# Gating the expert rows where they are made, with the gates carried in the rows of x, and a last stage that adds two gated rows

## The chip, the cores and the metric

One core of a Trainium2 chip. Its engines work side by side, each through its own list of instructions in order: PE (TensorE, matrix products into PSUM), DVE (VectorE), ACT (ScalarE), POOL (GpSimd) and SP, which here only starts transfers. Sixteen DMA engines move data between DRAM and the on-chip memory (SBUF). The time is device microseconds (us) of one execution, and a kernel's time is the median of its runs. Beside the runs there is one profiled execution, which gives the trace.

## The reference

Feature rows x of 6250 nodes (D = 256) go through a graph layer, a mixture of experts, a batch norm and a layer norm:

- x' = gc(x) + x W_res + b: each node sums the scaled rows of its neighbours over 200,000 edges, followed by a product with W_gc.
- Router: logits x' Wg + bg over 64 experts, the two largest, gates g0 and g1 = softmax of the two.
- Expert e on a row: h = gelu(row w1[e] + b1[e]) (512 wide), y = h w2[e] + b2[e] (256 wide).
- core(n) = g0 y0 + g1 y1 for the two experts of node n.
- v = x' + core; mean and variance of v over all nodes, per column; batch norm with gamma and beta.
- Output: layer norm, per row, of x + batchnorm(v).

All values are float32.

## The kernel before, in words

Nodes are numbered in 50 tiles of 125 (`NT`, `TP`). The stages in order:

1. **Graph stage**, to about 950 us: x' is made tile by tile and written to `x_dram` in DRAM; top-2 values and indices are kept in SBUF.
2. **Routing**, to about 1013 us. SP loads all of x' back into `x_all` (L1193, in tens of tiles), DVE makes the gates (L1240, L1241, `gates[:, 2, NT]`), and each token's place in its expert is counted. `table` builds, with one-hot products on PE, for each slot of each expert the token that sits there; `tokens` (L1355 to L1365) turns that into `ids` (the row of x' to fetch) and `dest` (the row of `y_dram` to write: 2 x token + which of its two experts). The gates are multiplied by `valid` (L1374).
3. **Expert stage**, to about 1475 us. 64 experts in turns, each with 80 to 416 slots, in blocks of 128 slots; 124 blocks in all. For a block POOL gathers rows of x' (`rows_in`, indirect DMA, four experts ahead), PE transposes them (`turned_in`), DVE adds a bias on the way out of PSUM (`xgT`), PE makes the first layer in four pieces (`ph`, 4 matmuls each), ACT applies Gelu (`hT`), PE makes the second layer (`py`, 8 matmuls for a block), DVE adds b2 (`ys`, L1462), and POOL scatters the rows to `y_dram` (L1463). SP loads the weights two to three experts ahead. PE, ACT, DVE and SP keep the order in which `slotted` writes the work down: per turn two pieces of the next expert's first layer, the transposes of the one after it, then blocks of the second layer and the remaining pieces in alternation. In each fourth turn DVE subtracts a column mean `c0` from four tiles of `x_all` (L1506), 13 times in all; this centres the batch norm's sums. POOL adds beta to rows of x meanwhile (L1513).
4. **Last stage.** `joined` loads, for two tiles at a time, the two expert rows of each token (`yr`, 2 KB a token, 8 buffers), ACT multiplies one by its gate (L1590), DVE multiplies the other and adds it to x (L1592), then adds the first (L1594). `summed` squares the result on ACT (L1599), and PE sums over the nodes with a matrix of ones: the values into `pm` (L1601), the squares into `pv` (L1603), two accumulations over all 50 tiles. Then come mean, variance and `scale` (L1613 to L1623), and the norm of the rows, group by group, with the stores of the output.

DRAM stores of 125 rows are cut in 112 and 13 rows by `node_dma`. All of the last stage stands in written order.

Of the kernel before, what the change touches and what calls it, by code (L numbers as in the profile page):

```python
# [25 lines left out]
N = 6250  # L26
# [37 lines left out]
OPENING = 40  # L64
SIZES_OUT = [1, 2, 3] + [6] * 6 + [4, 3, 1]
# [85 lines left out]
def gnn_moe_kernel(ctx, tc, x_in, x_cols, src, dst, bases, nexts, firsts, parts, lasts, W_gc, b_gc, W_res, b_res, Wg, bg, w1, b1, w2, b2,  # L151
# [53 lines left out]
    x_dram = dram.tile([N, D], F32, name="x_dram")  # L205
# [35 lines left out]
    with tc.tile_pool(name="edges", bufs=1) as ep, ExitStack() as later:  # L241
# [352 lines left out]
        with tc.tile_pool(name="xs", bufs=1) as xs, tc.tile_pool(name="hotg", bufs=2) as hg, \  # L594
# [246 lines left out]
            def x_step(c, t):  # L841
# [6 lines left out]
                if u == 0 and "x" in live:  # L848
                    t0, z, xr = live["x"]
                    live["steps"] = x_make(z, xr, 2, node_rows(x_dram, t0, 2))  # L850
# [172 lines left out]
            with tc.For_i(0, NT, 1) as ti:  # L1023
# [4 lines left out]
                for run in x_make(z, xr, 1, rows_at(x_dram)):  # L1028
                    run()
# [20 lines left out]
    gates = rpool.tile([TP, 2, NT], F32, name="gates")  # L1050
# [54 lines left out]
    with tc.tile_pool(name="xw", bufs=1) as xw, tc.tile_pool(name="xl", bufs=3) as xl, \  # L1105
# [42 lines left out]
        with tc.manual_schedule():  # L1148
# [38 lines left out]
            node_dma(nc.sync, False, x[:, ta:tb, :], node_rows(x_dram, ta, tb - ta))  # L1187
            for a, b in ((0, ta), (tb, NT)):
                for t0 in range(a, b, 10):
                    n = min(10, b - t0)  # L1190
                    node_in(x_all[:, t0:t0 + n, :], x_dram[:, :], t0, n, ta)
# [48 lines left out]
    V.tensor_mul(gates[:, 1, :], g2, g1)  # L1240
    V.tensor_copy(gates[:, 0, :], g1)  # L1241
# [113 lines left out]
    def tokens(pool, id_t, id_p, dump, n, ids, dest):  # L1355
# [7 lines left out]
        V.tensor_copy(ids, idp)  # L1363
        V.scalar_tensor_tensor(idp, idf, 0.0, dump, op0=ALU.is_equal, op1=ALU.mult)
        V.scalar_tensor_tensor(dest, idf, -1.0, idp, op0=ALU.add, op1=ALU.add)  # L1365

    with tc.tile_pool(name="rt2", bufs=2) as rt2, \
# [5 lines left out]
        for a, b, o in spans:  # L1373
            V.tensor_mul(gates[:, :, a:b], gates[:, :, a:b], valid[:, :, o:o + b - a])  # L1374
        tokens(rt, id_t, id_p, dump, COLS, ids, dest)
# [18 lines left out]
    with tc.tile_pool(name="ex", bufs=2) as xp, \  # L1394
# [33 lines left out]
        def turned_in(xgs, m):  # L1428
# [24 lines left out]
        def second_layer(w2s, b2s, hT, to, m, static):  # L1453

            def block(k):
                n = min(128, m - k * 128)
                py = ps_y.tile([128, D], F32, name="py")
                for c in range(4):
                    T.matmul(py[:n], hT[:, c, k * 128:k * 128 + n], w2s[:, c, :], start=(c == 0),  # L1459
                             stop=(c == 3))  # L1460
                ys = xp.tile([128, D], F32, name="ys", bufs=6)
                V.tensor_add(ys[:n], py[:n], b2s[:n])  # L1462
# [8 lines left out]
        def expert(at, idc, to, m):  # L1471
            w1s, b1_e = first_weights(at)
            w2s, b2s = second_weights(at)
            hT, pieces = first_layer(w1s, b1_e, turned_in(rows_in(idc, m, False), m), m)
            for run in pieces + second_layer(w2s, b2s, hT, to, m, False):
# [5 lines left out]

# [261 lines left out]
```

## Time and profile before

| | us |
|---|---|
| median of 3 runs | 1600.42 (1599.77 to 1601.79) |
| the profiled execution | 1588.94 |
| its span, first to last instruction | 1587.2 |
| PE busy | 1405.6 (89%) |
| DVE busy | 1039.2 (65%) |
| ACT busy | 734.7 (46%) |
| POOL busy | 784.7 (49%) |

The span is what the trace shows; the execution's own time is 1.7 us longer. A busy PE is one with a matmul under way, and matmuls overlap. In rows of the stretches each engine has its busy time and, in brackets, its number of instructions; PEclk is the granted share of TensorE's clock, the DMA share is that of the 16 DMA engines, and the last figure is GB/s. In rows of groups stand line, engine, operation, output and inputs, shape and count, then busy time and the mean of one in ns, and behind the second bar the idle time ahead of them with who ended it. In rows of the timeline: start, duration, engine, line, and in brackets the idle time before. PEld is PE's loading of weights, SPq an instruction of SP's list.

### The profile page before, as it was taken

To read this page: it belongs to the slowest core of one execution; us is meant where nothing else is said; L and a number is where in the kernel's file an instruction comes from. 1 tells how busy PE (TensorE), PEld (TensorE's weight loads), DVE (VectorE), ACT (ScalarE), POOL (GpSimd) and SP (SyncE) were. 2 spreads that over 40 slices of the span, in tenths; PEclk is the share of its full clock that TensorE was granted. 3 is DMA by queue.
4 is the path that set the end of the run, shared out by engine and by line. 5 is a ranking of instruction groups with operands and counts; after the bars stand their busy time and mean duration, and the time that the engine had idled before them with its cause. 6 is when DMAs were issued, how large, how long until landed. Compare 5 with 4: busy or idle time off the path is not lost. (4 is left out here: it accounts for less than half of the span.)

```text
span 1587.2 us, 33048 instructions
## 1 busy us (share of the span) xinstructions
PE 1405.6 (89%) x9969; PEld 1156.2 (73%) x9969; DVE 1039.2 (65%) x2926; ACT 734.7 (46%) x1884; POOL 784.7 (49%) x883
## 2 busy tenths in 40 slices
PE   5999478888899999999999976689999999999893
PEld 2555367777778888999999975678788877777661
DVE  8999988788788887887777738522222233222687
ACT  3676543355555556565555533322222222222667
POOL 5000226766666666666667621255556666554000
PEclk8999699999999999999999996799999999999987
DMA  6899655767677777787777738176678787686725
GB/s 185 263 283 328 238 180 165 198 185 202 186 200 213 214 196 220 200 217 201 219 207 208 215 108 283 55 239 214 224 230 265 255 263 255 202 247 212 265 86 152
DMA packets 209124, 336.40 MB, mean 212 GB/s; under 512 B 22259, under 2 KB 140693, under 8 KB 208937
## 3 DMA queue, kind: packets, MB, share of 16 engines
q1 hardware_dynamic: 154084, 180.30, 36.1%
q0 software_dynamic: 47952, 146.83, 32.6%
q10 hardware_dynamic: 6900, 7.07, 1.6%
q8 instruction: 81, 1.33, 0.4%
q14 instruction: 107, 0.87, 0.2%
HBM read 254.55 MB, written 73.10 MB: 206 GB/s over the span
## 5 line engine op out<-in xcount | busy, mean ns | idle before, releaser
L614 POOL DMA_INDIRECT r<-h_dram,srcg x445 | 474.1, 1065 | 277.9 <-PE pc L700 99.0
L746 PE MATMUL sm<-hrow,counts 128*128 128x258 f32 x1470 | 489.9, 347 | 10.4 <-DVE counts L737 10.2
L720 ACT CAST counts<-pc 128x196 f32 (+7 forms) x879 | 356.6, 406 | 255.3 <-PE pc L700 134.4
L747 PE MATMUL sm<-hrow,counts 128*128 128x256 f32 x1470 | 396.8, 283 | 0.0
L700 PE MATMUL pc<-hotk,lo 128*128 128x245 bf16 (+7 forms) x1118 | 305.3, 304 | 55.6 <-DVE counts L737 17.7
L746 PEld LDWEIGHTS sm<-hrow,counts 128*128 128x128 f32 x1470 | 288.5, 196 | 37.4 <-issue 19.9
L687 DVE TENSOR_TENSOR hotk<-key,iota_h 128x784 bf16<-128x784 f16 (+4 forms) x488 | 247.5, 507 | 87.4 <-PE pc L700 50.8
L747 PEld LDWEIGHTS sm<-hrow,counts 128*128 128x128 f32 x1470 | 281.9, 192 | 1.3
L1449 ACT ACTIVATE hT<-ph,b1c 128x112 f32<-128x112 f32 (+16 forms) x256 | 106.8, 428 | 348.7 <-PE ph L1447 236.2
L737 DVE TENSOR_TENSOR counts<-pc,counts 128x49 f32 x908 | 217.9, 240 | 52.9 <-issue 10.2
L1459 PE MATMUL py<-w2s,hT 128*128 128x256 f32 (+7 forms) x992 | 241.2, 386 | 0.1
L1447 PE MATMUL ph<-xgT,w1s 128*128 128x112 f32 (+17 forms) x1024 | 207.3, 346 | 11.9 <-issue 9.4
L1447 PEld LDWEIGHTS ph<-xgT,w1s 128*128 128x128 f32 x1024 | 169.8, 194 | 44.4 <-issue 22.7
L1459 PEld LDWEIGHTS py<-w2s,hT 128*128 128x128 f32 (+7 forms) x992 | 162.7, 172 | 43.7 <-issue 3.6
L1412 POOL DMA_INDIRECT y_dram<-ys,dest x124 | 119.2, 961 | 138.9 <-DVE ys L1462 77.2
L1462 DVE TENSOR_TENSOR ys<-py,b2s 128x256 f32<-128x256 f32 (+7 forms) x124 | 51.8, 421 | 165.3 <-PE py L1459 112.6
L700 PEld LDWEIGHTS <-lo 128*128 128x128 bf16 x1118 | 100.8, 101 | 80.9 <-issue 22.4
L1437 DVE TENSOR_SCALAR xgT<-pte,bsum 128x112 f32<-128x112 f32 (+14 forms) x128 | 48.9, 424 | 167.4 <-PE pte L1434 74.2
L619 PE MATMUL pg<-r,hot 128*128 128x258 f32 x445 | 145.7, 328 | 12.4 <-issue 9.2
L1412 POOL DMA_INDIRECT xg<-x_dram,ids x124 | 119.3, 962 | 41.4 <-issue 26.7
L620 PE MATMUL pg<-r,hot 128*128 128x256 f32 x445 | 125.9, 283 | 0.0
L619 PEld LDWEIGHTS pg<-r,hot 128*128 128x128 f32 x445 | 86.0, 193 | 22.2 <-issue 17.3
(332 smaller groups left out, 1728.7 us busy)
## 6 DMA issues: line engine op xcount, KB each, us to landing
w1s<-in_L_gnn_w_dram SPq DMA_DIRECT2D x64, 512.0 KB
w2s<-in_L_gnn_w_dram SPq DMA_DIRECT2D x64, 512.0 KB
y_dram<-zeros SPq DMA_DIRECT2D x48, 256.0 KB
yr<-y_dram SPq DMA_DIRECT2D x22, 512.0 KB
b2s<-in_L_gnn_b_dram SPq DMA_DIRECT2D x64, 128.0 KB
h_dram<-hrow SPq DMA_DIRECT2D x5, 1536.0 KB
r<-h_dram,srcg POOLq DMA_INDIRECT x445
f<-in_x_cols_dram SPq DMA_DIRECT2D x25, 256.0 KB
```

What stands on the lines that cost most here:

```text
L614: G.indirect_dma_start(out=f32(r[:, :2 * D]), out_offset=None, in_=h_dram[:, :], in_offset=bass.IndirectOffsetOnAxis(ap=idx, axis=0))
L619: T.matmul(pg, hot, r[:, D:], start=first, stop=False)
L620: T.matmul(pg[:, :D], hot, r[:, :D], start=False, stop=last)
L687: V.tensor_tensor(hot, pairs(key, e, n, m), iota_h[:, None, :m, :].to_broadcast([128, n // 2, m, 2]), ALU.is_equal)
L700: T.matmul(pc, los[g // PAIRS][:, r // 2, :, r % 2], hots.pop(g), start=(i == 0), stop=(i == k - 1))
L720: put = S.copy(counts[c % 2][:, :, 1:][:, :, ds(at, w - 1)], pc[:, :, 1:])
L737: add = V.tensor_tensor(to, more, f32(had), ALU.add).ins
L746: T.matmul(sm, by, hrow[:, t, D:], start=(t == 0), stop=False)
L747: T.matmul(sm[:, :D], by, hrow[:, t, :D], start=False, stop=(t == NS - 1))
L1412: w = G.indirect_dma_start(**kw)
L1447: T.matmul(ph[:, :m], w1s[:, kk, c * 128:(c + 1) * 128], xgT[:, kk, :m], start=(kk == 0), stop=(kk == 1))
L1459: T.matmul(py[:n], hT[:, c, k * 128:k * 128 + n], w2s[:, c, :], start=(c == 0), stop=(c == 3))
```

## The change

- `x_dram` gets two columns more: a row is 258 floats. Once the gates are made (now `[125, NT, 2]`), SP stores them from SBUF into these columns, one DMA of 125 x 50 pieces of 8 bytes. Reads and writes of x' use the first 256 columns. The gather of a block brings 258 floats.
- `tokens` also makes `mine_of`: for each slot two 0/1 numbers that say whether it is the token's first or second choice (one product and two comparisons on DVE). The multiplication of the gates by `valid` goes.
- `turned_in` makes, per block, the slot's gate as the sum of the two carried gates times those two numbers (one small DVE instruction with an accumulator).
- `second_layer`: DVE adds b2 (into `yb`), ACT multiplies by the slot's gate into `ys`, which is scattered, and DVE adds the gated rows to `y_sum` (one tile of 128 x 256 for all blocks).
- In each fourth turn DVE also adds the centred tiles of x into `x_sum` (4 tiles wide); at turn 52 `x_sum` is folded into `y_sum`. POOL zeroes both beforehand.
- Last stage: `pm` is one matmul over `y_sum`, and `mean` and `msq` are made ahead of the loop. `joined` takes groups of 1, 1, 2, eleven times 4, and 2 tiles (4 buffers of 4 tiles), with one DMA for each (the last group has its last tile apart), and only adds the two rows to x, on DVE. `summed` squares a group on ACT and sums the squares on PE, in the same turn as its group.

```diff
+SIZES_IN = [1, 1, 2] + [4] * 11 + [2]
-    x_dram = dram.tile([N, D], F32, name="x_dram")
+    x_dram = dram.tile([N, D + 2], F32, name="x_dram")
+    x_rows = x_dram[:, :D]
...
-    V.tensor_mul(gates[:, 1, :], g2, g1)
-    V.tensor_copy(gates[:, 0, :], g1)
+    V.tensor_mul(gates[:, :, 1], g2, g1)
+    V.tensor_copy(gates[:, :, 0], g1)
+    w = nc.sync.dma_start(out=node_rows(x_dram[:, D:], 0, NT), in_=gates)
+    for u in loads:
+        tc.declare_no_dep(w.ins, u.ins, reason="other columns of x_dram")
+    G.memset(y_sum, 0.0)
+    G.memset(x_sum, 0.0)
...
         V.tensor_copy(ids, idp)
+        odd = pool.tile([128, n], F32, name="odd")
+        V.scalar_tensor_tensor(odd, idp, -2.0, idf, op0=ALU.mult, op1=ALU.add)
         V.scalar_tensor_tensor(idp, idf, 0.0, dump, op0=ALU.is_equal, op1=ALU.mult)
         V.scalar_tensor_tensor(dest, idf, -1.0, idp, op0=ALU.add, op1=ALU.add)
+        for j in range(2):
+            V.tensor_scalar(mine[:, :, j], odd, float(j + 1), None, op0=ALU.is_equal)
...
-        for a, b, o in spans:
-            V.tensor_mul(gates[:, :, a:b], gates[:, :, a:b], valid[:, :, o:o + b - a])
...
-                xg = gx.tile([128, D], F32, name="xg")
+                xg = gx.tile([128, D + 2], F32, name="xg")
...
+            for k, xg in enumerate(xgs):
+                n = min(128, m - k * 128)
+                two = gx.tile([128, 2], F32, name="two")
+                V.scalar_tensor_tensor(two[:n], xg[:n, D:], 1.0, mine[k][:n], op0=ALU.mult, op1=ALU.mult,
+                                       accum_out=gate[k][:n])
             return xgT
...
+                yb = xp.tile([128, D], F32, name="yb", bufs=3)
+                V.tensor_add(yb[:n], py[:n], b2s[:n])
                 ys = xp.tile([128, D], F32, name="ys", bufs=6)
-                V.tensor_add(ys[:n], py[:n], b2s[:n])
+                S.activation(ys[:n], yb[:n], AF.Copy, scale=gate[k][:n])
+                V.scalar_tensor_tensor(y_sum[:n], yb[:n], gate[k][:n], y_sum[:n], op0=ALU.mult, op1=ALU.add)
...
                     V.tensor_tensor(xs, xs, c0[:, None, :].to_broadcast([TP, min(4, NT - e), D]), ALU.subtract)
+                    V.tensor_tensor(x_sum[:, :min(4, NT - e)], x_sum[:, :min(4, NT - e)], xs, ALU.add)
+                if e == NT + 2:
+                    V.tensor_tensor(x_sum[:, :2], x_sum[:, :2], x_sum[:, 2:], ALU.add)
+                    for j in range(2):
+                        V.tensor_tensor(y_sum[:TP], y_sum[:TP], x_sum[:, j], ALU.add)
...
-    with tc.tile_pool(name="fin", bufs=1) as fp, tc.tile_pool(name="gat", bufs=8) as gp, \
+    with tc.tile_pool(name="fin", bufs=1) as fp, tc.tile_pool(name="gat", bufs=4) as gp, \
...
+        T.matmul(pm, ones[:, :TP], y_sum, start=True, stop=True)
         mean = fp.tile([TP, D], F32, name="mean")
         V.tensor_scalar(mean, pm, 1.0 / N, None, op0=ALU.mult)
         msq = fp.tile([TP, D], F32, name="msq")
         V.tensor_mul(msq, mean, mean)
+
+        def joined(t0, n):
+
+            yr = gp.tile([128, 4, 2, D], F32, name="yr")
+            loads.clear()
+            node_in(yr[:, :n].rearrange("p t j d -> p t (j d)"), y_rows, t0, n)
+            for u in written[-AHEAD:-1] if t0 == 0 else ():
+                tc.add_manual_dep(loads[0].ins, u.name, SYNCED, reason="the last writes")
+            for j in range(2):
+                V.tensor_tensor(x[:, t0:t0 + n, :], x[:, t0:t0 + n, :], yr[:TP, :n, j, :], ALU.add)
+
+        def summed(t0, n):
+
+            sq = fl.tile([TP, 6, D], F32, name="o")
+            S.activation(sq[:, :n], x[:, t0:t0 + n, :], AF.Square)
+            for t in range(t0, t0 + n):
+                T.matmul(pv, ones[:TP, :TP], sq[:, t - t0, :], start=(t == 0), stop=(t == NT - 1))
+
+        t0 = 0
+        for n in SIZES_IN:
+            joined(t0, n)
+            summed(t0, n)
+            t0 += n
```

The old `joined` and `summed`, with the gate multiplications and the 50 matmuls into `pm`, go.

More of the change, by code (lines that the diff above doesn't have):

```diff
@@ L1027, in gnn_moe_kernel @@
                 z, xr = x_load(rows_at(z_dram), rows_at(r_dram), 1)
-                for run in x_make(z, xr, 1, rows_at(x_dram)):
+                for run in x_make(z, xr, 1, rows_at(x_rows)):
                     run()
@@ L1049, in gnn_moe_kernel @@
     dest = rpool.tile([128, COLS], I32, name="dest")
-    gates = rpool.tile([TP, 2, NT], F32, name="gates")
+    gates = rpool.tile([TP, NT, 2], F32, name="gates")
+    mine_of = rpool.tile([128, COLS, 2], F32, name="mine_of")
+    gate_of = rpool.tile([128, COLS], F32, name="gate_of")
+    y_sum = rpool.tile([128, D], F32, name="y_sum")
+    x_sum = rpool.tile([TP, 4, D], F32, name="x_sum")
     c0 = rpool.tile([TP, D], F32, name="c0")
@@ L1353, in table, with tokens @@
                     T.matmul(id_p, q_p[:, i // 2, :, i % 2], cols[:, i // 2, :, i % 2], **edge)
-    def tokens(pool, id_t, id_p, dump, n, ids, dest):
+    def tokens(pool, id_t, id_p, dump, n, ids, dest, mine):
         idp = pool.tile([128, n], F32, name="idp")
@@ L1372, in gnn_moe_kernel @@
         table(rt2, id_t, id_p, blk_b, COLS)
-        for a, b, o in spans:
-            V.tensor_mul(gates[:, :, a:b], gates[:, :, a:b], valid[:, :, o:o + b - a])
-        tokens(rt, id_t, id_p, dump, COLS, ids, dest)
+        tokens(rt, id_t, id_p, dump, COLS, ids, dest, mine_of)
         pn = ps_l.tile([128, 1], F32, name="pn")
@@ L1451, in first_layer, with second_layer @@
             return hT, [lambda c=c: piece(c) for c in range(4)]
-        def second_layer(w2s, b2s, hT, to, m, static):
+        def second_layer(w2s, b2s, hT, to, gate, m, static):
             def block(k):
@@ L1469, in second_layer, with expert @@
             return [lambda k=k: block(k) for k in range(len(to))]
-        def expert(at, idc, to, m):
+        def expert(at, idc, to, mine, m):
+            gate = [xp.tile([128, 1], F32, name="gate_e")]
             w1s, b1_e = first_weights(at)
             w2s, b2s = second_weights(at)
-            hT, pieces = first_layer(w1s, b1_e, turned_in(rows_in(idc, m, False), m), m)
-            for run in pieces + second_layer(w2s, b2s, hT, to, m, False):
+            hT, pieces = first_layer(w1s, b1_e, turned_in(rows_in(idc, m, False), m, mine, gate), m)
+            for run in pieces + second_layer(w2s, b2s, hT, to, gate, m, False):
                 run()
@@ L1480, in columns, with turned @@
             return [tab[:, c + k:c + k + 1] for k in range(n)]
+        def turned(e, xgs):
+            c, n, m = _place(turns[e])
+            return turned_in(xgs, slots_of_turn[e], [mine_of[:, c + k, :] for k in range(n)], columns(gate_of, e))
         slots_of_turn = [_place(r)[2] for r in turns]
```

56 lines of the change are left out of this document (18 added, 38 removed).

## The prediction

> **What bounds the kernel now.** I read the page first (which engine is full), then the busy time by stretches (which engine is full where), the chain that ended last (what sets the end of the last stage), the groups of that stage, and the timeline around the two seams. The change touches three places: the routing that ends near 1015 us, the expert stage up to 1475 us, and the first part of the last stage.
>
> ```profile
> span 1587.2 us, 33048 instructions
> ...
> core 0: us, PE busy (x) PEld busy (x) DVE busy (x) ACT busy (x) POOL busy (x), PEclk, DMA share, GB/s
> 1000.00:1005.00 5.00, 3.14 (x41) 2.87 (x40) 5.00 (x8) 3.35 (x3) 0.00 (x0) 0.85 0.00 0
> 1100.00:1470.00 370.00, 364.41 (x1892) 292.83 (x1891) 100.43 (x270) 86.94 (x212) 217.26 (x213) 0.99 0.75 237
> 1478.00:1488.00 10.00, 7.96 (x18) 4.18 (x18) 4.08 (x9) 4.94 (x10) 0.00 (x0) 0.66 0.78 245
> 1488.00:1498.00 10.00, 9.41 (x44) 8.22 (x45) 9.28 (x19) 9.54 (x22) 0.00 (x0) 1.00 1.05 392
> 1498.00:1508.00 10.00, 10.00 (x48) 8.72 (x47) 9.37 (x20) 8.93 (x20) 0.00 (x0) 1.00 1.05 387
> 1508.00:1518.00 10.00, 10.00 (x48) 8.72 (x47) 9.37 (x20) 9.04 (x20) 0.00 (x0) 1.00 0.86 290
> 1518.00:1528.60 10.60, 10.60 (x50) 9.20 (x50) 5.30 (x11) 5.00 (x11) 0.00 (x0) 1.00 0.01 2
> ```
>
> Routing (1000 to 1005) is full on DVE, the expert stage (1100 to 1470) on PE with DVE 27% and ACT 23% busy, and the joining of the two expert rows of each token (1488 to 1528.6) is full on PE from 1498 on. There, though, nothing is far behind: DVE and ACT are 90% busy and the DMA engines saturated at 390 GB/s until the reads run out. The chain confirms that PE ends it:
>
> ```profile
> 1475.05 2.69 DMA y_dram<-ys,dest
> ...
> 1481.24 5.84 DMA yr<-y_dram
> ...
> 1490.58 0.86 PE pv L1603 x4
> ...
> 1527.70 0.88 PE pm L1601 x4
> 1528.60 0.43 DVE mean L1613
> 1529.06 0.43 DVE msq L1615
> 1529.60 0.44 DVE scale L1617
> ```
>
> Two tiles cost 0.86 us in `pm` and 0.86 in `pv`, taking turns to the end. The 50 tiles are 25 such pairs: 25 x 1.72 = 43 us of PE.
>
> **The join, part by part.** The rows that carry the terms:
>
> ```profile
> L1592 DVE SCALAR_TENSOR_TENSOR x_all<-yr,gates,x_all 125x256 f32<-125x256 f32 x50 | 21.9, 479 | 4.7 <-DMA yr<-y_dram 4.7
> L1594 DVE TENSOR_TENSOR x_all<-x_all,yr 125x512 f32<-125x512 f32 x25 | 17.3, 692 | 2.6
> L1590 ACT ACTIVATE yr<-yr,gates 125x256 f32<-125x256 f32 x50 | 22.6, 496 | 4.5 <-DMA yr<-y_dram 4.3
> L1599 ACT ACTIVATE sq<-x_all 125x512 f32<-125x512 f32 x25 | 15.7, 627 | 4.3 <-DVE x_all L1594 2.1 <-PE pv L1603 1.8 <-DVE x_all L1592 0.3
> L1639 DVE TENSOR_TENSOR x_all<-x_all,scale 125x1024 f32<-125x1024 f32 x1 | 1.2, 1216 | 0.0
> ```
>
> PE loses `pm` for all tiles but one matmul on `y_sum`, and keeps 25 x 0.86 = 21.5 us. ACT loses the 50 gate multiplications (22.6) and keeps the squares (15.7, less in larger pieces). DVE trades 21.9 + 17.3 = 39.2 us for two additions a group: 2 x 1.216 = 2.43 for each of the 11 groups of four, 2 x 0.69 for each of the two groups of two, 2 x 0.43 (the chain's 256-wide rows) for each of the two single tiles, 31.2 in all. So PE goes from 43 to 21.5, ACT from 38 to 16, DVE from 39 to 31. What is late next is the DMA. By the stretches it moved 2.45 + 3.92 + 3.87 + 2.90 = 13.1 MB from 1478 on; at 390 GB/s the 2.90 MB behind 1508 take 7.4 us, so the last row landed near 1515.4. A group of four is 128 x 4 x 2 KB = 1.05 MB, 2.69 us at that rate, against DVE's 2.43, so DVE keeps up. Four buffers of four tiles hold what eight of two held. A buffer comes free 2.5 us after its group has landed, while three groups (8 us) are still queued, so the reads don't starve.
>
> The end then follows from the last landing. The expert stage ends 0.5 us later (below), which puts it at 1515.9; larger first loads may win up to 1 us of the slow start (245 GB/s in 1478 to 1488), which I keep for the range. The last group (two tiles, 0.51 MB) lands 1.3 us behind its predecessor, so that one landed at 1514.6. DVE adds it until 1517.0 and the last until 1518.4. The square of four (about 0.9 to 1.05, estimated from L1599's 0.627 for half as much) is done by 1518.0, its four matmuls at 1.72 by 1519.8, the last square by 1519.1, the last two matmuls by 1520.7. `mean` and `msq` have been made long before, from `y_sum`, so `scale` starts at 1520.8 instead of 1529.60: 8.8 us sooner.
>
> That takes PE at full clock. PE would be busy 1.72 of each 2.69 us, 64%. The nearest row is 1000 to 1005, where PE is busy 3.14 of 5.00 us (63%) and the granted clock is 0.85, not 1.00. At 0.85 the last six tiles take 3.0 instead of 2.6 us; at half clock 5.2. I take 0.85, the row with the same load: 8.3 us sooner, with 6.2 as the bad end. The Trainium skill (TensorE: Matmul & The Clock Gate, Part 1: The HAM clock gate) says that the clock is halved only behind an idle window of about 3.4 us; PE would idle about 1 us at a time here, so by that rule it stays full and the gain is 8.8. The row of 1000 to 1005 speaks against it, and I go by the row.
>
> Everything behind `scale` stays as it is: the same chain, 58 us to the end.
>
> **The expert stage.** Each of the 124 blocks gets a second DVE pass over 256 (summed gated rows), a small DVE product with its accumulator, and an ACT multiplication between DVE and the scatter; 13 times DVE adds four tiles of x into `x_sum` behind the subtraction that is there already.
>
> ```profile
> L1462 DVE TENSOR_TENSOR ys<-py,b2s 128x256 f32<-128x256 f32 x69 | 29.2, 423 | 83.3 <-PE py L1459 62.1 <-PE ph L1447 13.4 <-issue 4.6
> L1506 DVE TENSOR_TENSOR x_all<-x_all,c 125x1024 f32<-125x1024 f32 x12 | 14.6, 1215 | 0.0
> L1217 DVE COPY b1c<-b1T 128x4 f32 x60 | 11.1, 184 | 4.9 <-issue 1.2 <-ACT hT L1449 0.5
> ...
> L1459 PE MATMUL py<-w2s,hT 128*128 128x256 f32 x528 | 129.9, 390 | 0.0
> ...
> L1447 PE MATMUL ph<-xgT,w1s 128*128 128x160 f32 x80 | 13.2, 303 | 0.0
> ...
> PEld py L1459 <- DVE ys L1462: 1.2, 5, 0.4
> ...
> PE ph L1447 <- ACT hT L1449: 1.8, 3, 0.8
> ```
>
> On DVE: 124 x (0.48 by L1592 + 0.25, estimated from the 0.18 of L1217 and an accumulator read) + 13 x 1.2 = 106 us; on ACT 124 x 0.50 by L1590 = 62 us. Spread over 450 us this takes DVE from 27 to about 50% and ACT from 23 to 37%: there is room, and PE's waits for both were 3 us in the whole stage. What counts is order. DVE and ACT work in order, so a scaled row that waits for DVE holds the next Gelu behind it on ACT, and PE waits for that Gelu one turn later. A block of `py` is 8 matmuls, 129.9 / 528 x 8 = 2.0 us; a piece of `ph` is 4, 13.2 / 80 x 4 = 0.7 us at 160 rows. In an ordinary turn DVE has two `xgT` (about 0.9 us, estimated as two passes like L1462's) and 2 x 0.25 us to do behind the transposes, and is ready before the first `py` ends: no loss. In each fourth turn it also has 1.2 + 1.2 us; the row of the first `py` is then made at about 4.2 to 4.6 us from the transposes, scaled at 5.1, and the two Gelus queued behind it are done at 5.9. PE asks for them behind its `py`, `ph` pieces (two of this turn, two of the next) and transposes: with two blocks 2 x 2.0 + 4 x 0.7 + about 0.4 = 7.2 us, with one block 5.2, and then it loses up to 0.7 to 1.2 us (the pieces of a small expert are shorter). 18 of 64 turns have one block, so about 4 of the 13 heavy turns: at most 4.8, and I take 1.5 us. The bounds are nothing (all hidden) and 13 x 1.2 = 15.6 (each addition shows in full); I stay near the low end because PE's waits for DVE were 1.2 us although the subtraction of the same length stood in that place. POOL's scatters start about 0.6 us later each, its gathers are four turns ahead, so nobody waits for that but the end: the last scatter has ACT's 0.50 in its path, the 0.5 us of above.
>
> **Routing and the gate store.**
>
> ```profile
> 977.12 0.35 SPq L189 DMA_DIRECT2D x_all<-x_dram  x1
> ...
> 978.20 0.41 SPq L1215 DMA_DIRECT2D w1s<-in_L_gnn_w_dram  x1
> ...
> 1012.29 0.23 DVE L159 TENSOR_SCALAR idp<-idp 128x124 f32<-128x124 f32 x1
> ...
> 1012.81 0.29 DVE L1364 SCALAR_TENSOR_TENSOR idp<-idf,dump 128x124 f32<-128x124 f32 x1
> ...
> 1013.57 0.24 POOL L1389 TENSOR_SCALAR below<-pidx 128x1 f32<-128x1 f32 x1 [53.87 <-DVE dest L1365]
> ...
> 1014.85 1.06 POOL L1412 DMA_INDIRECT xg<-x_dram,ids  x1 [0.17 <-issue]
> ...
> L1374 DVE TENSOR_TENSOR gates<-gates,valid x3: 161/197/203, 985.7 to 993.0; 125x48 f32<-125x48 f32 x1, 125x44 f32<-125x44 f32 x1, 125x8 f32<-125x8 f32 x1
> ...
> q1 hardware_dynamic: 430, 0.08, 20.3%
> ...
> q10 hardware_dynamic: 260, 0.26, 15.2%
> ```
>
> POOL starts the gathers behind DVE's last step of `tokens`; that gets `odd` (0.29) and two comparisons (0.23 each), 0.75 us, and DVE, which is full here, loses the three products of L1374, 0.56 us: +0.2. The two memsets on POOL lie in its 53.87 us of idleness.
>
> The gates go to DRAM as 6250 pieces of 8 bytes, on SP's queue between the last load of x (977.12) and the first weights (978.20), and every gather now waits until they have landed. The trace has no such store. The row of 430 packets (the 2 us from 24 us on, nearly all under 512 bytes, reads) gives 20.3% of 32 engine-us = 6.5, 15 ns a packet. The row of 260 (the 5 us from 1013, two loads of 125 rows of 1 KB with ten packets more, which I read as five engines reporting for each load) gives 15.2% of 80 = 12.2, 47 ns a packet. On five engines the store has 1250 packets each: 19 us by the first row, 59 by the second; on 16 it would be 6. I take 19, the row of like size. With 4 to 5 us of loads ahead of it, it ends near 1001, 13 us before the first gather asks; the first three experts' weights behind it (3.4 MB, about 9 us) land by 1010 and are wanted from 1020 on. Cost 0 then, and 24 us if a piece costs 47 ns (end at 1039).
>
> **Sum.** -8.3 (join, with the late last scatter in it) + 1.5 (expert stage) + 0.2 (routing) = -6.6 us. The profiled execution took 1588.94 us (span 1587.2 and 1.7 around it), so 1582.3 in its terms; the median of the runs was 1600.42, 11.5 above that one execution, and I carry the difference over: 1593.8.
>
> **Rivals.** (1) PE's clock: PE runs the join at half clock for most of it. Two tiles then take 1.72 us in `pv` alone, 43 us as before, and only the halves at full clock gain. For: 0.66 in 1478 to 1488, 0.85 at 63% load. Against: a PE that falls behind is busy without pause, and at 100% the rows show 1.00. With half the stretch slow, the join gains 4: about 1598. (2) The gate store is late. The Trainium skill (DMA: Bandwidth & Descriptors, Specifications) says that under 512 bytes the DMA engine reads, modifies and writes; nothing shown here has such a store. The place is the first gather at 1014.85, and the point from which it decides is 26 ns a piece ((1014.85 - 982) / 1250); from 31 ns on the kernel is slower. At 47 ns it costs 24 us: 1618. For: both bounds lie around that point. Against: the 4- to 256-byte packets of the trace cost 15. (3) DVE and ACT show in the expert stage: every heavy turn loses 1.2 us, 15.6 us instead of 1.5: 1608. For: PE is 98% busy, so each wait counts. Against: the two waits above, and DVE half idle.
>
> **Chances.** Forecast 0.65, rival 1 0.12, rival 2 0.13, rival 3 0.10. The forecast's own range is 1590 (start-up gained, expert stage free, full clock) to 1597.5. The whole range, 1588.5 to 1602.5, takes in rival 1 and leaves out most of rivals 2 and 3. 0.2% (3.2 us) is about what a measurement of this kernel can tell from no change. Faster by more: 0.60 of the forecast, 0.06 of rival 1, a little of rival 3's mild end; slower: most of rivals 2 and 3.
>
> **What would show it.** Right: no `pm` of 50 tiles, reads near 390 GB/s from start to end of the join, `scale` some 8 us sooner after the last scatter than 1529.60 - 1475.05 = 54.6 us, PE idle between groups. Gathers that start within 1 us of 1014.85 clear the store; PE's waits for DVE and ACT in the expert stage under 5 us clear that. Wrong: a pause on POOL before the first gather, `pv` at 0.8 us a tile, or the stage from the first gather to the last scatter longer than 460 us by more than 5.

## The result and the profile after

The changed kernel takes 1618.56 us (1613.30 to 1622.69, 5 runs) against 1600.42 (1599.74 to 1605.62, 5 runs): 1.0104 times the time before, with a 95% interval of 1.0084 to 1.0123. It is 18 us slower where 6.6 us of gain were forecast. Its profiled execution took 1618.23 us. The profiled execution of before (1588.94) lay 11.5 us under its own median, so the stages below are also held against a second profile of the kernel before, of 1600.75 us, from the experiments (`same_before`). (Of the executions in the experiments one, of `spread_3`, took 2260.56 us at a granted clock of 0.555, and its ratio leaves it out.) The three marks of `same_before`, from the timeline (first gather, last scatter, `scale`):

```profile
1027.19 1.06 POOL L1412 DMA_INDIRECT xg<-x_dram,ids  x1 [0.16 <-issue]
...
1485.83 0.86 POOL L1412 DMA_INDIRECT y_dram<-ys,dest  x1 [0.85 <-DVEq L1534]
...
1541.37 0.42 DVE L1617 SCALAR_TENSOR_TENSOR scale<-pv,msq 125x256 f32<-125x256 f32 x1
```

The seams of the changed kernel, in the same view: the gate store, the first weight load behind it, and the end of the routing.

```profile
992.42 0.29 SPq L1249 DMA_DIRECT2D x_dram<-gates  x1
993.49 16.21 SPq L1222 DMA_DIRECT2D w1s<-in_L_gnn_w_dram  x1
...
1028.82 0.25 POOL L1403 TENSOR_SCALAR below<-pidx 128x1 f32<-128x1 f32 x1 [53.01 <-DVE mine_of L1381]
...
1030.10 1.06 POOL L1426 DMA_INDIRECT xg<-x_dram,ids  x1 [0.17 <-issue]
```

SP stands for 16 us in the issue behind the store, whose 6250 packets run from 995.9 to 1011.0 us, 19 us ahead of the first gather. POOL waits for DVE's last step (`mine_of`), not for a transfer: the store holds nothing up here. Then the busy time by stretches, the expert stage first and then the join:

```profile
span 1616.6 us, 33281 instructions
...
1030.10:1509.30 479.20, 449.23 (x2264) 357.64 (x2264) 217.54 (x714) 155.90 (x381) 270.55 (x260) 0.97 0.71 221
1512.00:1522.00 10.00, 6.04 (x9) 2.60 (x10) 2.41 (x8) 1.90 (x3) 0.00 (x0) 0.66 0.61 212
1522.00:1532.00 10.00, 8.84 (x20) 5.68 (x20) 8.98 (x10) 3.68 (x5) 0.00 (x0) 0.51 1.01 358
1532.00:1542.00 10.00, 8.36 (x36) 6.30 (x35) 9.18 (x8) 3.71 (x4) 0.00 (x0) 0.98 1.05 386
1542.00:1552.00 10.00, 6.56 (x28) 4.54 (x26) 7.56 (x7) 3.42 (x4) 0.00 (x0) 1.00 1.00 356
```

The expert stage in `same_before`, in the same view:

```profile
1027.00:1486.00 459.00, 441.13 (x2264) 355.30 (x2264) 122.03 (x326) 107.13 (x257) 266.09 (x262) 0.98 0.73 230
```

From first gather to last scatter the expert stage takes 479.2 us, where before took 460.2 and, in `same_before`, 458.6: 20 us are lost here, with DVE only 45% busy. Some 8 of them are longer busy time of PE, 12 are idle time (30.0 instead of 17.5 us). The join is no longer full on PE, and its transfers run at 356 to 386 GB/s, except in the first ten microseconds (212). The chain shows what holds them up:

```profile
1509.34 2.93 DMA y_dram<-ys,dest
1512.27 1.47 issue
1513.74 5.34 PE pf L1610 x6
1519.08 0.45 PE pm L1616 x2
...
1519.55 0.44 DVE mean L1618
...
1520.01 0.42 DVE msq L1620
1520.43 0.35 DVE x_all L1630
...
1521.26 4.92 DMA yr<-y_dram
...
1558.91 0.44 DVE scale L1648
```

DVE, in order, makes `mean` and `msq` ahead of the first addition, and they wait for `pm` behind six `pf` matmuls. So the first addition comes 11.0 us behind the last scatter, and no buffer is free before it. In `same_before` it came 6.3 us behind the last scatter:

```profile
1492.17 0.48 DVE L1592 SCALAR_TENSOR_TENSOR x_all<-yr,gates,x_all 125x256 f32<-125x256 f32 x1 [2.47 <-DMA yr<-y_dram]
```

`scale` starts 49.6 us behind the last scatter instead of 55.5: 6.0 us of gain (5.0 against the first profile of before, with 54.6). From there to the end nothing changed (57.6 and 57.7 us). The groups, with the sizes of the new instructions:

```profile
L1483 ACT ACTIVATE ys<-yb,gate_of 128x256 f32<-128x256 f32 x69 | 35.1, 508 | 140.6 <-DVE yb L1481 109.6 <-issue 28.4 <-DVE two L1455 1.6
L1484 DVE SCALAR_TENSOR_TENSOR y_sum<-yb,gate_of,y_sum 128x256 f32<-128x256 f32 x69 | 33.5, 486 | 2.4
...
L1630 DVE TENSOR_TENSOR x_all<-x_all,yr 125x1024 f32<-125x1024 f32 x22 | 26.9, 1225 | 4.6 <-DMA yr<-y_dram 4.2
...
L1535 DVE TENSOR_TENSOR x_sum<-x_sum,x_all 125x1024 f32<-125x1024 f32 x12 | 14.7, 1225 | 0.5
```

Each is as long as it was costed (0.50, 0.48, 1.22). And the waits of PE (total in us, times, longest):

```profile
PEld py L1478 <- ACT hT L1468: 12.7, 11, 5.1
...
PE py L1478 <- ACT hT L1468: 8.3, 5, 4.7
...
PEld py L1478 <- DVE yb L1481: 3.2, 7, 1.0
```

PE now waits for Gelu's result in front of `py`. The first two rows in `same_before`:

```profile
PEld py L1459 <- ACT hT L1449: 3.8, 3, 2.6
...
PE py L1459 <- ACT hT L1449: 2.6, 3, 2.2
```

Behind such waits its clock is halved for a while (28 us of the stage instead of 15, which makes 0.97 instead of 0.98 in the mean), so that its busy time grows too, from 441.1 in `same_before` to 449.2 us.

### The profile page after: what moved, and what is told of

Same layout as the page of the kernel before. It is cut to its first block, busy times and chain, and to the rows that moved or that the text cites. A ratio compares the mean times of both kernels' runs of the same rounds, so it can differ in the third digit from the quotient of the medians.

```text
span 1616.6 us, 33281 instructions
## 1 busy us (share of the span) xinstructions
PE 1398.0 (86%) x9871; PEld 1137.2 (70%) x9871; DVE 1126.6 (70%) x3269; ACT 760.5 (47%) x1948; POOL 791.4 (49%) x885
## 5 line engine op out<-in xcount | busy, mean ns | idle before, releaser
L748 PE MATMUL sm<-hrow,counts 128*128 128x258 f32 x1470 | 489.8, 347 | 15.6 <-DVE counts L739 12.5
L1478 PE MATMUL py<-w2s,hT 128*128 128x256 f32 (+7 forms) x992 | 246.8, 391 | 18.3 <-ACT hT L1468 8.3
L1483 ACT ACTIVATE ys<-yb,gate_of 128x256 f32<-128x256 f32 (+7 forms) x124 | 63.0, 508 | 236.8 <-DVE yb L1481 177.8
L1481 DVE TENSOR_TENSOR yb<-py,b2s 128x256 f32<-128x256 f32 (+7 forms) x124 | 52.1, 420 | 128.5 <-PE py L1478 77.7
L1468 ACT ACTIVATE hT<-ph,b1c 128x112 f32<-128x112 f32 (+16 forms) x256 | 100.9, 420 | 86.2 <-PE ph L1466 41.1
L1451 DVE TENSOR_SCALAR xgT<-pte,bsum 128x112 f32<-128x112 f32 (+14 forms) x128 | 48.8, 423 | 128.7 <-PE pte L1448 47.5
```

Of the source, the lines that this page charges most:

```text
L748: T.matmul(sm, by, hrow[:, t, D:], start=(t == 0), stop=False)
```

## The experiments

Two kinds of chips turned up, and the numbers can't be read without that: on some (that of the result above and two others) the kernel before takes 1600 to 1603 us, on another 1531 to 1532. Each ratio is to the kernel before on the same chip. The table has the time of each run, its ratio with interval, and from its profile (whose own time stands first) the stages: start of the first gather, from there to the last scatter, from there to `scale`.

| kernel | time | ratio (95%) | profile | gather at | expert | to scale |
|---|---|---|---|---|---|---|
| *before at 1600 to 1603* | | | | | | |
| before | 1600.42 | | 1588.94 | 1014.85 | 460.2 | 54.6 |
| same_before | 1600.86 | 1.0000 (0.9982-1.0017) | 1600.75 | 1027.19 | 458.6 | 55.5 |
| after | 1618.56 | 1.0104 (1.0084-1.0123) | 1618.23 | 1030.10 | 479.2 | 49.6 |
| no_x_sum | 1610.27 | 1.0041 (1.0022-1.0060) | 1610.73 | 1029.80 | 471.4 | 49.2 |
| late_scale | 1605.48 | 1.0018 (0.9996-1.0039) | 1606.68 | 1030.73 | 467.1 | 49.4 |
| late_mean | 1618.77 | 1.0102 (1.0073-1.0131) | 1620.37 | 1030.13 | 483.2 | 47.5 |
| early_gate_3 | 1607.68 | 1.0030 (1.0010-1.0049) | 1604.53 | 1031.11 | 465.2 | 48.8 |
| spread_3 | 1611.60 | 1.0054 (1.0035-1.0073) | 1610.72 | 1030.72 | 471.9 | 49.2 |
| all_three_2 | 1597.58 | 0.9970 (0.9951-0.9989) | 1601.44 | 1027.38 | 467.6 | 47.3 |
| *before at 1531 to 1532* | | | | | | |
| same_before_2 | 1532.21 | 1.0002 (0.9989-1.0015) | 1532.03 | 978.20 | 440.7 | 54.0 |
| wide_rows | 1531.46 | 1.0001 (0.9991-1.0011) | 1533.51 | 979.03 | 440.8 | 54.2 |
| wide_rows_2 | 1532.04 | 1.0000 (0.9986-1.0014) | 1531.22 | 977.42 | 440.4 | 54.0 |
| same_after | 1527.59 | 0.9973 (0.9962-0.9984) | 1531.48 | 978.75 | 444.6 | 48.9 |
| early_gate | 1527.52 | 0.9978 (0.9966-0.9990) | 1529.22 | 979.25 | 440.9 | 49.8 |
| early_gate_2 | 1527.38 | 0.9968 (0.9953-0.9984) | 1530.21 | 980.74 | 441.1 | 49.3 |
| spread | 1529.05 | 0.9987 (0.9976-0.9997) | 1530.28 | 980.04 | 441.6 | 49.6 |
| spread_2 | 1528.25 | 0.9973 (0.9961-0.9985) | 1531.79 | 982.32 | 440.8 | 49.2 |
| late_scale_no_x_sum | 1527.77 | 0.9976 (0.9963-0.9989) | 1528.68 | 979.35 | 441.2 | 48.8 |
| no_y_sum | 1529.80 | 0.9981 (0.9970-0.9993) | 1527.70 | 977.11 | 440.5 | 49.3 |
| all_three | 1525.09 | 0.9950 (0.9932-0.9968) | 1525.09 | 977.11 | 440.0 | 48.0 |

**The kernel before, again (`same_before`).** No edit.

> The kernel before, unchanged, for a second profile. The profiles shown so far put its first gather at 1014.85 us, and that of the changed kernel at 1030.10, though the graph stage is hardly touched. Theory 1 (the one profiled execution of before was a quick one; it lay 11.5 us under its own median): the first gather now comes at 1022 to 1028, the stage from first gather to last scatter again takes 458 to 463 us, and 112 us follow. Theory 2 (the wider rows of x cost the graph stage 15 us): the first gather stays within 3 us of 1015.

The first gather came at 1027.19: the quick profile of before had its 12 us in the graph stage, and the change's 15 us of delay there were mostly that. Theory 1 holds. What is left is 2.9 us, of which the routing (from the last copy of the gates to the first gather) has 42.1 - 41.3 = 0.8; the other 2.1 lie ahead of it and were not explained. With 20.6 more in the expert stage and 6.0 less behind it, the 2.9 make up the 17.5 us between the two profiled executions.

**Without the additions into x_sum (`no_x_sum`).**

```diff
-                    V.tensor_tensor(x_sum[:, :min(4, NT - e)], x_sum[:, :min(4, NT - e)], xs, ALU.add)
```

> The changed kernel without the 13 additions of centred tiles into x_sum, so the mean lacks x (that part of the computation is left out). Theory A (the third rival of the prediction: DVE's second long instruction in each fourth turn delays the rows, ACT and then PE): the stage from first gather to last scatter falls from 479 to 464 to 467 us, and the time by 12 to 15, to about 1605. Theory B (what costs is the gate multiplication that stands ahead of a Gelu on ACT in every block): at most 3 us go, 1615 to 1619. Theory C (DVE's and ACT's added instructions cost little, and the difference is the spread of the graph stage): no change.

Theory A asked for 12 to 15 us off the stage and got 8; the time is 1.0041 of before instead of 1.0104. The long stretch on DVE is a cause, and not the only one.

**The gate multiplication behind the next Gelu (`late_scale`).** A block is cut in two, and its second half (ACT's multiplication, DVE's sum, the scatter) is written behind the next piece.

```diff
+                return lambda: gated(k, n, yb, ys)
+
+            def gated(k, n, yb, ys):
                 S.activation(ys[:n], yb[:n], AF.Copy, scale=gate[k][:n])
...
-                    for run in second[k:k + 1] + first[2 + k:3 + k]:
+                    late = [run() for run in second[k:k + 1]]
+                    for run in first[2 + k:3 + k]:
+                        run()
+                    for run in late:
                         run()
```

> The changed kernel with ACT's gate multiplication of a block, DVE's sum and the scatter written behind the next piece's Gelu instead of ahead of it; nothing is left out. Theory B (a Gelu waits on ACT behind a scaled row, which waits for DVE): PE's waits of 20 us for hT in the expert stage fall to about 5, the stage from 479 to about 465 us, the time to 1603 to 1607. Theory A (DVE's long instructions): the row is late all the same, and the Gelu gets ahead of it only in the heavy turns; a gain of 3 to 8 us, since in those turns too the Gelu no longer waits. Theory C: no change.

The stage fell to 467.1 and the time to 1605.48, as theory B had it, though every instruction is still there. In the waits of this kernel PE's for Gelu went from 12.7 and 8.3 us to:

```profile
PEld py L1478 <- ACT hT L1468: 5.2, 5, 1.6
...
PE py L1478 <- ACT hT L1468: 3.1, 4, 1.2
```

So the larger cause is ACT's order: the Gelu that PE needs stood behind a row that DVE had not yet made.

**`mean` and `msq` behind the first four tiles (`late_mean`).**

```diff
-        T.matmul(pm, ones[:, :TP], y_sum, start=True, stop=True)
-        mean = fp.tile([TP, D], F32, name="mean")
-        V.tensor_scalar(mean, pm, 1.0 / N, None, op0=ALU.mult)
-        msq = fp.tile([TP, D], F32, name="msq")
-        V.tensor_mul(msq, mean, mean)
...
             summed(t0, n)
             t0 += n
+            if t0 == 4:
+                T.matmul(pm, ones[:, :TP], y_sum, start=True, stop=True)
+                mean = fp.tile([TP, D], F32, name="mean")
+                V.tensor_scalar(mean, pm, 1.0 / N, None, op0=ALU.mult)
+                msq = fp.tile([TP, D], F32, name="msq")
+                V.tensor_mul(msq, mean, mean)
```

> The changed kernel with the matmul into pm, mean and msq moved behind the first four tiles of the join; nothing is left out. Theory D (DVE, in order, waits for pm, which stands behind six pf matmuls at half clock, before its first addition, and the four buffers then hold up the reads): the first addition comes at about 6.5 us from the last scatter's start instead of 11.1, and the last scatter to scale takes 46 to 47 us instead of 49.6; time 3 to 4 us less, about 1615. Rival: the first reads or the rate of 390 GB/s set the end, and nothing is gained.

The timeline of this kernel (last scatter, first addition, `scale`), and the first ten microseconds of its reads:

```profile
1513.37 0.86 POOL L1426 DMA_INDIRECT y_dram<-ys,dest  x1 [0.93 <-DVEq L1567]
...
1520.12 0.88 DVE L1625 TENSOR_TENSOR x_all<-x_all,yr 125x256 f32<-125x256 f32 x2 [1.99 <-DMA yr<-y_dram]
...
1560.90 0.42 DVE L1649 SCALAR_TENSOR_TENSOR scale<-pv,msq 125x256 f32<-125x256 f32 x1 [2.79 <-PE pv L1632]
```

```profile
1516.00:1526.00 10.00, 6.57 (x12) 2.92 (x12) 3.14 (x7) 2.95 (x5) 0.00 (x0) 0.66 0.75 260
```

The first addition now waits for its transfer (6.75 us behind the scatter), the reads run at 260 instead of 212 GB/s, and `scale` comes at 47.5 instead of 49.6. Theory D holds in its place with 2.0 us, short of its price (46 to 47). The time doesn't show it: the interval of four runs (1.0073 to 1.0131) is too wide for 2 us, and the expert stage of this profile was 4 us longer, which nothing in the edit explains.

**Both edits of the expert stage (`late_scale_no_x_sum`), and the rows and the store alone (`wide_rows`, `wide_rows_2`).** The latter is the kernel before with the wide rows and the store alone; `pair` is a copy of the gates made for the store:

```diff
-    x_dram = dram.tile([N, D], F32, name="x_dram")
+    x_dram = dram.tile([N, D + 2], F32, name="x_dram")
...
+    V.tensor_mul(pair[:, :, 1], g2, g1)
+    V.tensor_copy(pair[:, :, 0], g1)
+    w = nc.sync.dma_start(out=node_rows(x_dram[:, D:], 0, NT), in_=pair)
...
-                xg = gx.tile([128, D], F32, name="xg")
+                xg = gx.tile([128, D + 2], F32, name="xg")
```

> Both edits at once: the gate multiplication behind the next Gelu, and no additions into x_sum (the mean lacks x: that part is left out). Alone they took the expert stage from 479 to 467 and to 471 us. If the two are separate costs (12 and 8 us), the stage comes back to 459 to 460, that of before, and the time to about 1597. If they are one cost that shows twice (a late row of a heavy turn holding up a Gelu), the stage stays at 465 to 467 and the time at 1603 to 1605.

> The kernel before with only the 1032-byte rows of x_dram, the gathers of 258 floats and the store of the gates in 6250 pieces; the carried gates are read by nobody, and all else is as before. Theory W (wider rows cost: writes of x in the graph stage, unaligned reads in the expert stage): the first gather some 2 to 3 us later than 1027.2, the expert stage up to 4 us longer than 458.6, time 1604 to 1608. Rival (rows and store are free, as the prediction had it): within 1.5 us of the kernel before.

> The kernel before with the rows of 1032 bytes and the store of the gates alone, for a run beside a kernel before of about 1600 us. The changed kernels reached the last step of the gates at 985.8 to 989.7 us there, the kernel before at 973.0 and 985.9. Theory W (wider rows cost where the pauses are): gates at 988 to 990, 1.0015 to 1.003 of the kernel before. Rival (rows and store are free, as beside 1531): 0.999 to 1.001.

All three fell on the quicker chip. There rows and store are free (1.0001 and 1.0000), as forecast; beside 1600 they were not measured. With both edits the expert stage took as long there as that of the kernel with wide rows (441.2 and 440.8). That doesn't tell two separate costs from one that shows twice, for perhaps nothing is lost there even without the edits. The next run asks that.

**The changed kernel again (`same_after`).** No edit.

> The changed kernel, unchanged. In the first profiles SP's plain register instructions (0.01 to 0.05 us as a rule) took over 0.3 us in 32 to 47 of 365 cases of the expert stage, with all engines late around them; in the profiles of wide_rows, early_gate and spread, where the kernel before took 1531 us, none did, and the stage took 441 us instead of 459. Theory P (the change's longer hand-over PE, DVE, ACT, PE costs time only where such pauses hit it): beside a kernel before of about 1531 us this one takes 0.997 to 1.000 of it, with an expert stage of 441 to 444; beside one of about 1600 us it takes 1.008 to 1.012 again. Rival (the order on ACT and DVE costs as such): 1.005 to 1.010 of the kernel before on either.

On the quicker chip the same change is faster: 0.9973 (0.9962 to 0.9984), 4.8 us, all of it from the join (54.0 to 48.9). The expert stage, 444.6 in a profile 3.9 us above the median of its runs, costs 0 to 4 us; 2.4 us of its profile's excess are PE's wait for the first gathered rows (10.1 instead of 7.7). Theory P holds there, and the result is its other half. PE has no wait for Gelu in front of `py` there; in the stage itself these are its largest wait for DVE and its only one for Gelu:

```profile
PEld py L1478 <- DVE yb L1481: 2.0, 8, 0.4
...
PEld ph L1466 <- ACT hT L1468: 0.5, 1, 0.5
```

The same turn in both shows why. On the quicker chip (transposes, `xgT`, the two long instructions, row, scaled row, Gelu, PE's next block):

```profile
1048.80 0.57 PE L1448 MATMUL pte<-ident,xg 128*128 128x128 f32 x4
...
1049.41 0.84 DVE L1451 TENSOR_SCALAR xgT<-pte,bsum 128x240 f32<-128x240 f32 x2 [2.03 <-PE pte L1448]
...
1050.33 1.22 DVE L1534 TENSOR_TENSOR x_all<-x_all,c 125x1024 f32<-125x1024 f32 x1
...
1051.58 1.22 DVE L1535 TENSOR_TENSOR x_sum<-x_sum,x_all 125x1024 f32<-125x1024 f32 x1
1052.73 0.42 DVE L1481 TENSOR_TENSOR yb<-py,b2s 128x256 f32<-128x256 f32 x1
...
1053.59 1.33 ACT L1468 ACTIVATE hT<-ph,b1c 128x352 f32<-128x352 f32 x3
...
1055.35 1.91 PE L1478 MATMUL py<-w2s,hT 128*128 128x256 f32 x8
```

and in the changed kernel of the result:

```profile
1100.23 0.57 PE L1448 MATMUL pte<-ident,xg 128*128 128x128 f32 x4
...
1103.99 0.84 DVE L1451 TENSOR_SCALAR xgT<-pte,bsum 128x240 f32<-128x240 f32 x2 [4.73 <-PE ph L1466]
...
1104.91 1.22 DVE L1534 TENSOR_TENSOR x_all<-x_all,c 125x1024 f32<-125x1024 f32 x1
1106.16 1.23 DVE L1535 TENSOR_TENSOR x_sum<-x_sum,x_all 125x1024 f32<-125x1024 f32 x1
...
1107.31 0.42 DVE L1481 TENSOR_TENSOR yb<-py,b2s 128x256 f32<-128x256 f32 x1
...
1108.17 1.68 ACT L1468 ACTIVATE hT<-ph,b1c 128x352 f32<-128x352 f32 x4
...
1108.76 0.93 PE L1478 MATMUL py<-w2s,hT 128*128 128x256 f32 x3 [0.93 <-ACT hT L1468]
```

From the transposes' end to `xgT` it is 0.04 us in the first and 3.2 us in the second, with DVE idle and the data ready (the profile names `ph` there, but what `xgT` reads are the transposes). From `xgT` to the Gelu both take 4.2 us. PE works on meanwhile; 4.2 us fit in its work, 7.4 don't. It is not one turn alone. Counted from the transposes' end, or from DVE's last instruction where that ends later, `xgT` came over 1 us late in 16 of the 63 turns of the changed kernel (up to 5.9 us), 4 of them turns with the long instructions and 12 without. In `same_before` it was 18 turns (up to 7.7), on the quicker chip none (0.04 us at most). So the pauses are not of the change's making: the kernel before has them as often, and what the change did is to make its chain too long for them.

**The gate multiplication out of the rows' path (`early_gate`, `_2`, `_3`).** ACT multiplies b2 by the gate at the start of the turn, and DVE makes the gated row in one instruction.

```diff
+            gb = []
+            for k in range(len(to)):
+                n = min(128, m - k * 128)
+                gb.append(xp.tile([128, D], F32, name="gb", bufs=6))
+                S.activation(gb[k][:n], b2s[:n], AF.Copy, scale=gate[k][:n])
...
-                yb = xp.tile([128, D], F32, name="yb", bufs=3)
-                V.tensor_add(yb[:n], py[:n], b2s[:n])
                 ys = xp.tile([128, D], F32, name="ys", bufs=6)
-                S.activation(ys[:n], yb[:n], AF.Copy, scale=gate[k][:n])
-                V.scalar_tensor_tensor(y_sum[:n], yb[:n], gate[k][:n], y_sum[:n], op0=ALU.mult, op1=ALU.add)
+                V.scalar_tensor_tensor(ys[:n], py[:n], gate[k][:n], gb[k][:n], op0=ALU.mult, op1=ALU.add)
+                V.tensor_add(y_sum[:n], y_sum[:n], ys[:n])
```

> The changed kernel with the gate multiplication taken out of the way of the rows: at the start of a turn ACT multiplies b2 by the gates (so many ACT instructions of the same size as now, but none waits for DVE), DVE makes the gated row from PSUM in one instruction (py x gate + that) and adds it to y_sum. Nothing is left out. Theory B (ACT's order): the stage comes to 460 to 466 us, the time to 1598 to 1605, even though DVE and ACT work as long as in the changed kernel. Rival (the amount of added work on DVE and ACT counts): as the changed kernel, 1615 to 1619.

> The changed kernel with the gate multiplication off the rows' path, a second time. Theory P with theory B: beside a kernel before of about 1600 us it takes 0.998 to 1.003 of it, with a stage of 460 to 466 us, since no Gelu stands behind a row; beside one of 1531 us 0.998 again. Rival (any added instruction on DVE and ACT is exposed by the pauses): 1.008 or more beside 1600.

> The gate multiplication off the rows' path, for a run beside a kernel before of about 1600 us. Theory B (a Gelu waits on ACT behind a row that waits for DVE): 0.998 to 1.003 of the kernel before, stage 459 to 466 us. Rival (any added instruction on DVE and ACT is exposed by the pauses): 1.008 or more. Beside 1531: 0.997 again.

The third run fell beside 1603: 1.0030, at the edge of what theory B gave and far from the rival's 1.008, with as much work on both engines as in the changed kernel (DVE 220.0 and 217.5 us in the stage, ACT 151.5 and 155.9). Some 12 us of the loss belong to ACT's order ((1.0104 - 1.0030) x 1603); `late_scale` gave 14.

**The work on x spread (`spread`, `_2`, `_3`).**

```diff
-                if e % 4 == 0 and e < NT:
-                    xs = x[:, e:min(e + 4, NT), :]
-                    V.tensor_tensor(xs, xs, c0[:, None, :].to_broadcast([TP, min(4, NT - e), D]), ALU.subtract)
-                    V.tensor_tensor(x_sum[:, :min(4, NT - e)], x_sum[:, :min(4, NT - e)], xs, ALU.add)
+                if 0 <= e < NT:
+                    xs = x[:, e:e + 1, :]
+                    V.tensor_tensor(xs, xs, c0[:, None, :].to_broadcast([TP, 1, D]), ALU.subtract)
+                    V.tensor_tensor(x_sum[:, e % 4:e % 4 + 1], x_sum[:, e % 4:e % 4 + 1], xs, ALU.add)
```

> The changed kernel with the work on x spread: one tile is centred and added to x_sum in each of the first 50 turns (0.43 + 0.43 us by rows of 256) instead of four in each fourth (1.22 + 1.23). Nothing is left out; DVE's sum is even a little larger. Theory A (the long stretch in one turn is what shows): the stage falls to 468 to 473 us and the time to 1606 to 1611. Rival (DVE's total work): no gain or a loss, 1617 to 1621.

> The changed kernel with the work on x spread over 50 turns, a second time. Theory A (the long stretch on DVE): beside a kernel before of about 1600 us 1.004 to 1.006 of it, as no_x_sum; beside one of 1531 us 0.999 again. Rival (DVE's total work): 1.010 or more beside 1600.

> The work on x spread over 50 turns, for a run beside a kernel before of about 1600 us. Theory A (the long stretch on DVE): 1.004 to 1.006 of the kernel before, as without the additions. Rival (DVE's total work counts): 1.010 or more. Beside 1531: 0.997 again.

1.0054 beside 1603, in theory A's range: 8 us, about as much as leaving the additions out, while DVE's total grew from 217.5 to 233.7 us. By the times it is the length of the stretch, not the sum. The way from there to PE is not shown: in this profile PE waits as long for Gelu in front of `py` as in the changed kernel (12.7 and 9.0 us), and of the 7.3 us that the stage lost 5.6 are PE's busy time, with 16 us at half clock instead of 28.

**Without y_sum (`no_y_sum`), and the kernel before a third time (`same_before_2`).**

```diff
-                V.scalar_tensor_tensor(y_sum[:n], yb[:n], gate[k][:n], y_sum[:n], op0=ALU.mult, op1=ALU.add)
```

> The changed kernel without DVE's 124 additions of gated rows into y_sum (the mean lacks the experts' part: that is left out). ACT's order and the additions into x_sum stay. Theory of the order (a Gelu behind a late row, a late row behind the long stretch): y_sum stands behind both and delays only the row of a following block by at most 0.5 us; at most 4 us go, 1.008 or more of the kernel before beside 1600. Rival (the number of added DVE instructions counts): 8 us or more go, 1.005 or less. Beside 1531: 0.997.

> The kernel before a third time, for the spread of its stages in a profile: beside 1600 the gates at 973 to 988 us, the stage from first gather to last scatter at 458 to 462 and the rest at 112 to 113. Beside 1531: gates near 937, stage near 441, rest near 112, those of the kernel with wide rows.

Both fell on the quicker chip, where there is nothing to find (0.9981). Whether DVE's second pass itself costs on the other chips stays open.

**All three edits (`all_three`, `_2`):** `early_gate`, `spread` and `late_mean` together.

> Three edits of the changed kernel at once: gate multiplication off the rows' path, the work on x spread, and mean and msq behind the first four tiles of the join. Nothing is left out. If the expert stage's cost is the order (theories A and B) and the last stage's is the wait of its first addition (theory D), the stage is that of the kernel before within 2 us and the last stage 7 to 8 us shorter than before: 0.995 to 0.997 of the kernel before on either kind of run. Rival (pauses expose every added instruction): 1.000 or more beside 1600.

> The three edits at once, a second time, for a run beside a kernel before of about 1600 us. Theories A and B (the order on DVE and ACT is all that the pauses expose): the expert stage takes 459 to 463 us there, the last stage 105 to 106, and the time is 0.995 to 0.998 of the kernel before. Rival (the pauses expose every added hand-over or instruction): the stage takes 466 or more, 1.000 or more. Beside a kernel before of 1531 us: 0.995 again, which tells nothing new.

0.9950 beside 1532 and 0.9970 (0.9951 to 0.9989) beside 1603: a version that beats both kernels on both kinds of chips. Beside 1603 its time is as forecast, its expert stage is not: 467.6 us where 459 to 463 were expected, in a profile 3.9 us above its median. In that profile PE still waits 10.2 us for Gelu, now in front of `ph` (3.7 in the changed kernel), so the pauses go on exposing some of the added work. The last stage gains 8 us in the profile and the whole 4.8 by the ratio, so some 3 us of the expert or graph stage stay unexplained.

## Why the prediction was wrong, point by point

**The step that failed: "In an ordinary turn DVE has two xgT ... and is ready before the first py ends: no loss", and with it the 1.5 us of the expert stage.** It measured 20 us. The path itself was named rightly (a scaled row that waits for DVE holds the next Gelu on ACT), and the durations were right. The slack was not: it was computed with every hand-over immediate. That holds on the quicker chip (0.04 us), and there the term is 0 to 4 us. On the chip of the result DVE's first hand-over of a turn is over 1 us late in 16 of 63 turns, in ordinary turns as in heavy ones. Apart, undoing ACT's order gave 12 us back and spreading DVE's long stretch 8. Together, with the 2 of `late_mean`, they gave 21 ((1.0104 - 0.9970) x 1603), so by the times the two make up the loss; the one profile of both still has 9 us of it in the expert stage. Shown is that the loss comes where hand-overs are late and goes when the order is undone; no run took the pauses away on the same chip.

The profile of before had the pauses in it: DVE was once idle for 9.3 us where the profile names no releaser, while PE ran out of work for 6.0, and PE was busy 443 of 460 us (on the quicker chip 435 of 441). The prediction read PE's 1.2 and 1.8 us of waits as proof of slack. They only said that the old, shorter chain just fitted.

**The third rival** had the right place and sign, and nearly the right time for the stage (15.6 for 20), but only the smaller half of the mechanism: the 13 additions cost 8 us, and ACT's order in all the turns 12. That its 15.6 came near 20 is luck.

**The join** was put at 8.3 us, with the late last scatter in it, and gave 5.5: 6.0 behind the last scatter, less the scatter's 0.5 (4.5 against the first profile of before). PE, ACT and DVE lost what was said, and the reads became the bound. What failed is that "`mean` and `msq` have been made long before": on DVE they stand ahead of the first addition, and `y_sum` is complete only when the stage ends. That wait costs 2.0 us (`late_mean`). The sentence that the reads don't starve fell with it. The rest, about 1 us, was not run down.

**PE's clock.** I took 0.85 for a PE that is 64% busy, from one row of the routing. The load doesn't give that: the same five microseconds of the routing in the changed kernel ran at full clock at this load.

```profile
1015.20:1020.20 5.00, 3.21 (x54) 2.87 (x53) 5.00 (x8) 2.73 (x3) 0.00 (x0) 1.00 1.04 364
```

So did 1542 to 1552 in the join, with PE busy 6.56 of 10 us. For these stretches the rule of the Trainium skill (TensorE: Matmul & The Clock Gate, Part 1: The HAM clock gate), that an idle window of about 3.4 us halves the clock, was the better guide, and the trace agrees with it there. At the start of the join it doesn't: 1522 to 1532 ran at 0.51, and PE's idle time just before was 2.2 us (1519.5 to 1521.7). What decides in between stays open. It cost nothing that shows, for the chain runs over the reads in that time. Rival 1, half clock for most of the join, did not happen.

**Routing and the gate store** were right: 0.8 us instead of 0.2 in the routing, and nothing for the store. Its packets took 15 us in all, near the 19 of the row of small reads, but partly by luck: a packet took 20 ns where 15 were taken, and about eight engines were at work where five were taken. Rival 2 did not happen; that its 1618 us is the time measured is chance. **The last scatter**, 0.5 us later, was right: from the row's start to the scatter it is 1509.34 - 1508.11 = 1.23 us, in `same_before` 0.69. **The 11.5 us carried over** from one execution to the median were right too: `same_before` has them in the graph stage.

Without the pauses the forecast's sum would have been near: -6.6 against the -4.8 measured on the quicker chip. In part that is luck too, since the join gave 5.1 us there instead of 8.3 and the expert stage took back less than the 1.5 allowed for.

## What to carry to other kernels

Where an engine that works in order makes both a result that the bounding engine needs soon and one that waits for a third engine, write the needed one first: here the same instructions in another order were worth 12 us on the slower chips, and cost nothing on the quicker. Small waits of a full engine don't say how much slack its helpers have: look for idle helpers whose data is ready, and cost a longer hand-over with such a pause in it. Break a long instruction on a helper into pieces, even if the sum grows (8 us here on the slower chips).

## What the runs showed of the hardware

Two kinds of chips: the unchanged kernel at 1601 and at 1532 us, its expert stage at 458.6 and 440.7, its first gather at 1027 and 978. The clock granted is nearly the same (0.98 and 0.99 in the stage). In the slower kind short register instructions of SP, which wait for nobody, take up to 1.4 us. For the move ahead of each first-layer weight load (minimum, median, maximum in ns), in the changed kernel on the slower chip:

```profile
L1222 SPq MOVE w1s<-in_L_gnn_w_dram x64: 3/29/712, 993.4 to 1487.2; - x64
```

and on the quicker:

```profile
L1222 SPq MOVE w1s<-in_L_gnn_w_dram x64: 29/29/38, 942.8 to 1401.2; - x64
```

Of SP's 365 such instructions in the expert stage 32 to 47 took over 0.3 us in every profile beside 1600, and none in any profile beside 1532, whichever the kernel. In the pauses looked at they come with ACT and DVE standing still, their data ready. Four turns have a late hand-over to `xgT` in all nine profiles beside 1600, whichever the kernel, so it isn't chance which turns are hit. More loading of instructions it is not: in the expert stage of the changed kernel the two instruction queues moved 18 and 23 packets on the slower chip and 19 and 23 on the quicker. What pauses, and whether SP's slow instructions are its cause or another mark of it, stays open: no run took the transfers or the weights' issues away.
